# A 3x2x3 block product for q, v and k of a head pair, in place of three two-level 2x2x2 products, from the fourth image on

## The chip, the core and the metric

The kernel runs on one core of a Trainium2 chip. The metric is the device time of one launch in microseconds (us), the median of several runs. The engines of the core work side by side, each through its own queue in order: TensorE (PE) multiplies, VectorE (DVE) and ScalarE (ACT) do elementwise work and empty PSUM, GpSimd (POOL) and SyncE (SP) mostly issue transfers (DMAs). All numbers are fp32.

## The reference

For each of 16 images `x` of 512 channels by 1024 positions:

```python
xn  = group_norm(x, 8 groups) * gamma + beta
qkv = einsum('oc,bchw->bohw', qkv_w, xn) + qkv_b     # 1536 x 512 weights
q, k, v -> 4 heads of 128 channels each
attn = softmax(q . k / sqrt(128))                    # 1024 x 1024 per head
out  = proj_w @ (attn . v) + proj_b                  # 512 x 512 weights
return x + out
```

Per image that is three products of 512 x 512 by 512 x 1024 for q, k and v, four heads of attention, and a fourth such product for the projection.

## The kernel before

**Steps and half steps.** The work is a row of 512 steps: image b, head h, step j of 8 (one block of 128 keys). A step has two halves of 512 queries. In each half PE does one score product (`score`, L1004, 128x512 columns), one weighted sum of the step before (`weighted_sum`, L1101, 128x512), and then the units of a linear product that `plan_head` (L1306) has laid into that half (`halfway`). ACT makes the exponentials (L1010), DVE adds them up for the denominators (`running_sum`, L1023 and L1025). What is made one image ahead: in head 2 of image b the q and k of heads 0 and 1 of image b+1, in head 3 its v, in head 0 of image b+1 the q and k of its heads 2 and 3, in head 1 the projection of image b.

**A linear product before.** `two_levels` (L608) applies a 2x2x2 scheme of 7 products (Winograd's form of Strassen's) twice. The outer level cuts 512 x 512 weights and 512 x 1024 data into 2 x 2 blocks of 256 x 256 and 256 x 512; `OUTER` orders its 7 products into groups of 2, 2, 2 and 1 that share PSUM banks. The inner level (`strassen`, L555) does each outer product as 7 products of 128 x 128 weights by 256 columns (L696, two instructions each, as for every fp32 product here). A unit is one inner product of the whole group; a group has 7 units, in the order p1, p2, p6, p5, p7, p4, p3. The q and k of a head pair are one such product (its weights are the 256 rows of q above the 256 of k), v another, the projection a third.

**Around the units.** Weights of a group come from DRAM by SP (`group_weights`, L429, two buffers of each of two tiles). The inner sums t1 to t4 of the data blocks are made by DVE for the first use (`make_sum`, L661), sent to DRAM by POOL (L667) and loaded again by SP for the two later products (L681, L764). PSUM is emptied by ACT copies (L569 for p1, u2 and u3, L723 for c21) and by DVE additions (L725 for c11, c22, c12). DVE then adds the outer results (L779), writes q and k with their bias (L860), or v with its bias (L918), which it transposes in 32 x 32 blocks (L921); v goes through DRAM by POOL to its last layout (L929, L934). Outer sums of the data are L346, for x and for the projection's input.

**Banks.** PSUM has two banks `x` and two `y` for the linear products, two for scores, two for the weighted sums. In a group p1, p6, p7 and p4 accumulate in one `x` bank, p2 has a `y` bank, p5 and p3 another; so p6 can start when ACT has copied p1, p7 when it has copied u2, p4 when it has copied u3, and p3 when DVE has made c22.

**Order.** The order of each engine's instructions is fixed when the program is built, from the order in which the code emits them and the priorities that it gives (`tc.high_priority`, `tc.issue_after`).

## Time and profile before

| | us |
|---|---|
| median of 3 runs (3135.09 to 3135.28) | 3135.15 |
| span of the profiled execution, first to last instruction | 3133.4 |
| PE busy in it | 3128.2 |
| DVE busy | 2671.6 |
| ACT busy | 1450.0 |
| POOL busy | 513.4 |

The profile page lists one execution. No time outside the first and the last instruction of that execution is given, so its own time is the span; the runs' median is 1.75 us above it. A row of a group has line, engine, operation, output<-input, shape and count, busy time and mean duration of one. A row of a timeline has the start in us, how long the merged instructions took, and their count; consecutive instructions of an engine overlap at their ends, so the distance from start to start is what one of them costs in a full queue. A row of a table by stretches has the busy time of PE, PE's weight loads, DVE, ACT and POOL, the granted clock, the share of the DMA engines and GB/s. One head of a middle image takes 48.6 us, one image 194.5 us.

### The profile page before, as it was taken

How to read it: one execution, taken by the hardware profiler on the slowest of the kernel's cores; microseconds unless marked ns; L12 is line 12 of the kernel's file. 1: busy time of each engine (PE TensorE's matmuls, PEld its weight loads, DVE VectorE, ACT ScalarE, POOL GpSimd, SP SyncE). 2: the span in 40 equal slices, each digit the busy share in tenths (PEclk: the TensorE clock that was granted, in tenths of full speed). 3: DMA queues.
4: the chain of work that ended last, by engine and by line, in shares of the span. 5: the costliest groups of instructions: out<-in, count | busy, mean ns of one | idle time of the engine just before them, and what ended most of it. 6: DMA issues, size and time to landing. Idle time of an engine off the chain costs nothing.

```text
span 3133.4 us, 34161 instructions
## 1 busy us (share of the span) xinstructions
PE 3128.2 (100%) x10418; PEld 2201.9 (70%) x10418; DVE 2671.6 (85%) x4721; ACT 1450.0 (46%) x2663; POOL 513.4 (16%) x923
## 2 busy tenths in 40 slices
PE   9999999999999999999999999999999999999999
PEld 7567777777777777777777777777777777777765
DVE  9988889788897888978799787997879978799787
ACT  3545435354354543545435454453534535345433
POOL 0121121111211112111121101212012120121200
PEclk9999999999999999999999999999999999999999
DMA  5554554545555455454554545555455554555641
GB/s 178 173 188 152 195 175 165 163 152 192 172 169 165 146 197 171 164 169 144 198 170 166 170 143 193 168 176 167 145 187 173 174 173 140 182 171 178 189 133 45
DMA packets 210362, 522.57 MB, mean 167 GB/s; under 512 B 32368, under 2 KB 65776, under 8 KB 210176
## 3 DMA queue, kind: packets, MB, share of 16 engines
q1 hardware_dynamic: 132320, 278.26, 28.7%
q0 software_dynamic: 65184, 207.75, 19.5%
q10 hardware_dynamic: 12672, 34.35, 3.3%
q8 instruction: 85, 1.39, 0.2%
q14 instruction: 101, 0.83, 0.1%
HBM read 387.07 MB, written 133.17 MB: 166 GB/s over the span
## 4 chain that ended last, share of the span: by engine, by line
PE 100%; DVE 0%; issue 0%
PE s L1004 28%; PE po L1101 28%; PE qk_x L696 12%; PE qk_y L696 9%; PE pp_x L696 6%; PE v_x L696 6%; PE pp_y L696 4%; PE v_y L696 4%; PE v_x L878 0%; PE warm L1393 0%; PE v_y L878 0%; PE lx L1208 0%; PE lv L1208 0%; PE v_z L878 0%; PE last_x L696 0%; PE lz L1208 0%
## 5 line engine op out<-in xcount | busy, mean ns | idle before, releaser
L1004 PE MATMUL s<-qk,qk 128*128 128x512 f32 x2048 | 1045.6, 592 | 0.0
L1101 PE MATMUL po<-p,v 128*128 128x512 f32 x2048 | 1045.4, 592 | 0.0
L1010 ACT ACTIVATE p<-s 128x512 f32<-128x512 f32 x1024 | 610.7, 596 | 877.5 <-PE s L1004 857.8
L1101 PEld LDWEIGHTS po<-p,v 128*128 128x128 f32 x2048 | 616.2, 301 | 375.2 <-issue 258.1
L1025 DVE TENSOR_TENSOR tot<-tot,p 128x1024 f32<-128x1024 f32 (+1 forms) x408 | 472.0, 1157 | 136.2 <-ACT p L1010 134.6
L1004 PEld LDWEIGHTS s<-qk,qk 128*128 128x128 f32 x2048 | 389.0, 190 | 68.9 <-issue 13.6
L696 PEld LDWEIGHTS qk_x<-qk_t,w 128*128 128x128 f32 x1344 | 254.9, 190 | 152.2 <-issue 95.2
L696 PE MATMUL qk_x<-qk_t,w 128*128 128x256 f32 x1344 | 352.4, 379 | 0.0
L569 ACT COPY qk_u<-qk_x 128x512 f32<-128x512 f32 (+1 forms) x256 | 136.4, 533 | 233.8 <-PE qk_x L696 232.7
L929 POOL DMA_DIRECT2D vd<-vu x120 | 66.6, 555 | 959.3 <-DVE vu L921 959.1
L725 DVE TENSOR_TENSOR qk_r<-qk_y,qk_u 128x512 f32<-128x512 f32 (+1 forms) x256 | 157.3, 615 | 35.0 <-ACT qk_u L569 21.8
L980 POOL DMA_DIRECT2D out_y<-y x120 | 65.4, 545 | 645.3 <-DVE groups L304 401.3
L725 DVE TENSOR_TENSOR v_r<-v_y,v_u 128x512 f32<-128x512 f32 (+1 forms) x120 | 75.8, 632 | 107.7 <-ACT v_u L569 77.4
L667 POOL DMA_DIRECT2D kept_t<-qk_t x240 | 130.2, 544 | 215.8 <-DVE qk_t L661 190.2
L696 PE MATMUL pp_x<-pp_t,w_proj 128*128 128x256 f32 x630 | 165.3, 379 | 0.0
L696 PE MATMUL v_x<-v_t,w_v 128*128 128x256 f32 x630 | 165.3, 379 | 0.0
L696 PEld LDWEIGHTS pp_x<-pp_t,w_proj 128*128 128x128 f32 x630 | 119.7, 190 | 62.5 <-issue 35.9
L696 PEld LDWEIGHTS v_x<-v_t,w_v 128*128 128x128 f32 x630 | 119.7, 190 | 59.0 <-issue 34.4
L934 POOL DMA_DIRECT2D v<-vd x240 | 140.4, 592 | 68.1 <-issue 37.5
L696 PE MATMUL qk_y<-x,w 128*128 128x256 f32 x512 | 142.1, 379 | 0.0
L860 DVE SCALAR_TENSOR_TENSOR qk<-qk_r,qkb_sb,qk_r 128x512 f32<-128x512 f32 x192 | 137.3, 743 | 1.7
L921 DVE STREAM_TRANSPOSE vu<-vt 128x512 f32<-128x512 f32 x120 | 134.7, 1123 | 0.8 <-DMA vd<-vu 0.8
(259 smaller groups left out, 4413.9 us busy)
## 6 DMA issues: line engine op xcount, KB each, us to landing
w<-kept SPq DMA_DIRECT2D x90, 512.0 KB, 3.9
kept_t<-qk_t POOLq DMA_DIRECT2D x180, 256.0 KB, 2.7
v_t<-kept_t SPq DMA_DIRECT2D x180, 256.0 KB, 2.8
w<-kept SPq DMA_DIRECT2D x90, 384.0 KB, 3.4
rinv<-row ACTq DMA_DIRECT2D x63, 512.0 KB, 4.7
x<-in_x POOLq DMA_DIRECT2D x60, 512.0 KB, 5.0
vd<-vu POOLq DMA_DIRECT2D x120, 256.0 KB, 2.8
v<-vd POOLq DMA_DIRECT2D x240, 128.0 KB, 4.0
```

The costliest lines, as they stand in the source:

```text
L569: nc.scalar.copy(t[n][:, :width], t["x"][:, :width])
L667: nc.gpsimd.dma_start(t, to)
L696: latest["product"] = nc.tensor.matmul(acc[:, ts(i, Q)], have["w"][t][:, i, slot, :], inner(i, bn), start=(first and i == 0), stop=True, s ...
L725: latest["outer"] = nc.vector.tensor_add(dst, view(a), view(c))
L860: return nc.vector.scalar_tensor_tensor(st[b, h][:, ts(half, HALF)], a, qkb_sb[:, i : i + 1], c, ALU.add, ALU.add)
L921: nc.vector.transpose(u.rearrange("p (q i j) -> p j q i", q=n, i=BLK), t.rearrange("p (j q i) -> p j q i", q=n, i=BLK),)
L929: nc.gpsimd.dma_start(rows[which][ts(h, P), :], u)
L934: nc.gpsimd.dma_start(vs[b, pair][ts(q, BLK), half].rearrange("m h (k i) j -> m (h k) (i j)", k=n), rows[which].rearrange("(k m) (q e) -> ...
L1004: latest["score"] = nc.tensor.matmul(sc, ks[b, h][:, ts(j, P)], qs[b, h][:, ts(half, HALF)], start=True, stop=True)
L1010: exps[s] = nc.scalar.activation(ps[s][:, ts(half, HALF)], sc, AF.Exp, scale=SCALE)
L1025: added[b, h, j] = nc.vector.tensor_add(tot[b, h][:, i], tot[b, h][:, i], ps[s][:, i])
L1101: summed = nc.tensor.matmul(po[half], v_block(b, h, j), ps[s][:, i], start=(j == 0), stop=(j == NB - 1),)
```

## The change

For images 3 to 15 (`OLD = 3`) the new function `thirds(b)` takes the place of `qk_groups` and `v_groups`. For each of the two head pairs the 256 rows of q, of v and of k are three blocks of weights over two blocks of inner channels (3 x 2), and the image is two blocks of channels by three pieces of 342 columns that overlap by one column (2 x 3, starts 0, 341 and 682). A scheme of 15 outer products (`FORMS_A`, `FORMS_B`, and the sums in `combine`) stands for the 18 of the plain block product. Each outer product is done by the same inner `strassen` with columns of 171 in place of 256. The 15 are ordered in 8 groups (`THIRDS`: seven of 2, one of 1); two head pairs make 16 groups and 112 units, laid over 48 half steps, 2, 3 and 2 to a half, from head 2 of image b-1 to the end of head 0 of image b, and one unit in its head 1. Before, each of these heads had 28 units for its 16 half steps.

- DVE makes the sums of data blocks (`make_forms`) and the inner sums (`make_sum`) for pair 0, POOL sends both to DRAM, SP loads both for pair 1.
- ACT empties p1, u2, u3 and c21 as before; where a block carries a bias (`BIASED`) the group's copy is split in two instructions of 171.
- Sums of weights for the 15 products are made once (`lay_builder`, `form_steps`, `inner_steps`) during images 0 and 1, and those of pair 1 during image 3 (`sum_weights`).
- x, q and k tiles are joined in pairs, and the SBUF set aside for descriptors of DMAs is 4096 bytes a partition.

Images 0, 1 and 2, the projection and the attention are as before. Counted in the two programs, one middle image has 49 x 3 products of 256 columns for q, k and v before and 210 of 171 columns after. Its other instructions for q, k and v:

| engine, what | before | after |
|---|---|---|
| DVE sums of data blocks | 8 of 512 | 11 of 684 |
| DVE inner sums | 56 of 256 | 20 of 342, 20 of 171 |
| DVE emptying PSUM | 27 of 512, 9 of 256 | 42 of 342, 6 of 171 |
| DVE outer results | 9 of 1024 | 24 of 684 |
| DVE q and k written | 16 of 512 | 8 of 684 |
| DVE v with bias / transposed | 8 of 512 / 8 of 512 | 12 of 342 / 8 of 512 |
| ACT emptying PSUM | 36 of 512, 12 of 256 | 32 of 342, 56 of 171, and 8 of 342 that write q and k |
| sums and forms to DRAM, MB | 3.7 | 9.1 |
| the same loaded again, MB | 7.3 | 9.1 |
| weights loaded, MB | 9.6 | 13.8 |

The core of the diff:

```diff
+THIRDS = ((7, 8), (5, 2), (3, 4), (0, 1), (11, 6), (13, 10), (9,), (14, 12))
+W3 = 342
+S3 = (0, 341, 682)
+H3 = W3 // 2
...
+BIASED = {0: (0, -1), 5: (2, 1), 14: (0, 1), 12: (2, 1)}
+HOMES = "ABABABCABABABACB"
+OLD = 3
...
-    xpool = ctx.enter_context(tc.tile_pool(name="x", bufs=NCC))
+    xpool = ctx.enter_context(tc.tile_pool(name="x", bufs=KC))
-    qkpool = ctx.enter_context(tc.tile_pool(name="qk", bufs=4))
+    qkpool = ctx.enter_context(tc.tile_pool(name="qk", bufs=PAIRS))
-    opool = ctx.enter_context(tc.tile_pool(name="o", bufs=HEADS + 1))
+    opool = ctx.enter_context(tc.tile_pool(name="o", bufs=HEADS + 2))
...
+        def make_forms(G):
+            p, g = parts(G)
+            if p or g not in FORMS_B:
+                return
+            n = size(G)
+            forms[G] = tpool.tile([P, KC, 2, W3], F32, tag="f", bufs=3, name=f"f_{b}_{G}")
...
+            for i, (f, op, a, c) in enumerate(FORMS_B[g]):
+                made[f] = forms[G][:, :, i, :]
+                eng = nc.vector
+                (eng.tensor_add if op == "+" else eng.tensor_sub)(made[f], of(a), of(c))
...
+            nc.gpsimd.dma_start(t, forms[G][:, :, :n, :])
...
+        def load_sum(G, m):
+            g = G % count
+            nc.sync.dma_start(sum_tile(G, m), inner_kept[b, g, m])
...
+        def evict(dst, src, row, G):
...
+            if not any(f in BIASED for f in group):
+                nc.scalar.copy(dst, src)
+                return
+            for i, f in enumerate(group):
+                if f not in BIASED:
+                    nc.scalar.copy(dst[:, i, :], src[:, i, :])
+                    continue
+                m, sign = BIASED[f]
+                nc.scalar.activation(
+                    dst[:, i, :], src[:, i, :], AF.Identity, bias=column(m, p, row, sign)
+                )
...
+            def mm(acc, j, start):
+                an, bn = FACTORS[j]
+                t, slot = SLOTS[an]
+                for i in range(n):
+                    moving = sums[G, bn][:, i, :] if bn[0] == "t" else block(
+                        G, i, int(bn[1]) - 1, int(bn[2]) - 1
+                    )
+                    latest["product"] = nc.tensor.matmul(
+                        acc[:, ts(i, H3)], wts[G, t][:, i, slot, :], moving,
+                        start=(start and i == 0), stop=True, skip_group_check=True,
+                    )
...
+                after_(G + 1, 0, load_weights, 0)
+                after_(G + 1, 3, load_weights, 1)
+                after_(G, 0, sum_weights)
+                after_(G + 1, 1, make_forms)
+                after_(G + 1, 2, make_sum, "t1")
+                after_(G + 1, 3, make_sum, "t2")
+                after_(G + 1, 4, make_sum, "t3")
+                after_(G + 1, 5, make_sum, "t4")
+                after_(G + 2, 3, load_forms)
...
+        units = staggered(
+            [group_units(G) for G in range(2 * count)], [4 * G for G in range(2 * count)]
+        )
+        sizes = (2, 2) + (2, 3, 2) * 15 + (1, 2)
...
+        if flow and h != 1:
+            if h == 0:
+                late["heads"] = True
+            spread(plan, [None] * 37, 0, NB)
+            halfway.extend(flow[:16])
+            del flow[:16]
...
+        elif b + 1 >= old:
+            if h == 2:
+                flow.extend(thirds(b + 1))
+                spread(plan, [None] * 37, 0, NB)
+                halfway.extend(flow[:16])
+                del flow[:16]
...
-    nc = bacc.Bacc("TRN2", target_bir_lowering=False, num_devices=1)
+    nc = bacc.Bacc(
+        "TRN2", target_bir_lowering=False, num_devices=1, dynamic_dma_scratch_size=4096
+    )
```

## The prediction, as it was put on record

> **What bounds the kernel now.** I read the page first (busy times, slices, chain), then the table of waits of PE, then stretches of one head, then timelines for what one instruction costs.

> ```profile
> span 3133.4 us, 34161 instructions
> PE 3128.2 (100%) x10418; PEld 2201.9 (70%) x10418; DVE 2671.6 (85%) x4721; ACT 1450.0 (46%) x2663; POOL 513.4 (16%) x923
> PEclk9999999999999999999999999999999999999999
> PE 100%; DVE 0%; issue 0%
> PE s L1004 28%; PE po L1101 28%; PE qk_x L696 12%; PE qk_y L696 9%; PE pp_x L696 6%; PE v_x L696 6%; PE pp_y L696 4%; PE v_y L696 4%; PE v_x L878 0%; PE warm L1393 0%; PE v_y L878 0%; PE lx L1208 0%; PE lv L1208 0%; PE v_z L878 0%; PE last_x L696 0%; PE lz L1208 0%
> PE warm L1393 <- DVE avg L251: 1.6, 1, 1.6
> ```

> The chain is PE from end to end at full clock, and the last row is PE's whole table of waits: 1.6 us, at the start. So PE's own stream is the time, and whatever it loses or gains counts in full. But DVE is at 85%, so there is little room before it takes over. By head of one image (head 1, 2, 3 and the next image's 0), then the whole image, with columns PE, PE's loads, DVE, ACT, POOL, clock, DMA share, GB/s:

> ```profile
> 1055.90:1104.50 48.60, 48.60 (x164) 34.40 (x163) 43.18 (x87) 33.49 (x67) 4.41 (x8) 1.00 0.40 128
> 1104.50:1153.10 48.60, 48.60 (x163) 34.54 (x162) 44.92 (x80) 19.11 (x34) 10.76 (x20) 1.00 0.64 213
> 1153.10:1201.70 48.60, 48.60 (x163) 34.55 (x162) 33.94 (x53) 19.31 (x35) 4.41 (x8) 1.00 0.46 145
> 1201.70:1250.40 48.70, 48.70 (x164) 34.62 (x164) 43.65 (x73) 19.17 (x34) 13.17 (x24) 1.00 0.62 191
> 1104.50:1299.00 194.50, 194.50 (x649) 138.15 (x648) 165.67 (x290) 91.11 (x168) 32.73 (x59) 1.00 0.53 169
> ```

> DVE works 44.9 of 48.6 us in head 2 and PE still does not wait. That a queue at 92% holds nobody up is the best evidence for the order of this kernel.

> **PE's stream.** What one pass costs (an fp32 product is two passes), from start to start. First loads of weights and products in the opening, then a half step of image 5:

> ```profile
> 8.46 2.09 PEld L1393 LDWEIGHTS warm<-avg 128*128 128x128 f32 x18
> 10.47 0.30 PEld L1423 LDWEIGHTS pm<-mv,avg 128*128 128x128 f32 x2
> ...
> 25.37 7.07 PE L878 MATMUL v_x<-wv_a,xt 128*128 128x256 f32 x32
> 32.28 1.89 PE L878 MATMUL v_y<-wv_s,x 128*128 128x256 f32 x8
> ...
> 1163.44 1.02 PE L1004 MATMUL s<-qk,qk 128*128 128x512 f32 x2
> 1164.30 1.02 PE L1101 MATMUL po<-p,v 128*128 128x512 f32 x2
> ```

> 256 columns: (32.28 - 25.37) / 32 = 0.2159 us. 512 columns: 0.86 / 2 = 0.430. 128 columns: (10.47 - 8.46) / 18 = 0.1117, each with a load of its own. No row has 171 columns. From 256 and 512 a column costs (0.430 - 0.2159) / 256 = 0.00084, so 171 columns come to 0.2159 - 85 x 0.00084 = 0.145. The line between 128 and 256 gives 0.147, pure proportion 0.144. I take 0.145, because 128 columns may already be limited by the load. One image then has 210 x 2 x 0.145 = 60.9 us where it had 147 x 2 x 0.2159 = 63.5: 2.6 less, and 13 images (3 to 15) give **-33.5 us** (-22 by 0.147, -39 by 0.144). The saving is 4.6% of columns (35910 for 37632), and a fixed cost of 6 ns a pass would be enough to eat it.

> [...]

> **VectorE.** What its operations cost in a full queue:

> ```profile
> 1108.30 0.75 DVE L661 TENSOR_TENSOR qk_t<-x 128x256 f32<-128x256 f32 x2
> 1108.97 0.75 DVE L661 TENSOR_TENSOR qk_t<-x,qk_t 128x256 f32<-128x256 f32 x2
> ...
> 1137.15 1.22 DVE L1114 TENSOR_TENSOR o<-o,rinv 128x1024 f32<-128x1024 f32 x1
> 1138.29 1.22 DVE L779 TENSOR_TENSOR qk_r<-qk_r,qk_r 128x1024 f32<-128x1024 f32 x1
> 1139.42 0.68 DVE L346 TENSOR_TENSOR o<-o 128x512 f32<-128x512 f32 x1
> 1140.03 1.22 DVE L779 TENSOR_TENSOR qk_r<-qk_r,qk_r 128x1024 f32<-128x1024 f32 x1
> ...
> 1146.82 0.75 DVE L860 SCALAR_TENSOR_TENSOR qk<-qk_r,qkb_sb 128x512 f32<-128x512 f32 x1
> 1147.48 0.42 DVE L725 TENSOR_TENSOR qk_r<-qk_y,qk_p 128x256 f32<-128x256 f32 x1
> ```

> 256 elements 0.335, 512 0.60, 1024 1.135, and 512 with a bias 0.66. By lines between them 684 is 0.78, 342 is 0.424 (0.484 with bias) and 171 is 0.247. With the counts of the two programs, before: 8 x 0.60 + 56 x 0.335 + (27 x 0.60 + 9 x 0.335) + 9 x 1.135 + 24 x 0.66 = 68.8 us an image. After: 11 x 0.78 + 20 x 0.424 + 20 x 0.247 + (42 x 0.424 + 6 x 0.247) + 24 x 0.78 + 8 x 0.78 + 12 x 0.484 = 72.0. So +3.2, 168.9 us of an image of 191.9. That does not bound the image, but its spread changes: bias and copies of q and k move from the ends of products into the flow, and sums of blocks pile up in head 2, where the pair 0 forms are made. Adding these costs along the changed program's DVE queue gives for heads 0 to 3 41.4, 44.8, 46.5 and 32.5 us, beside PE's 46.3, 49.8, 48.9 and 46.9. The same sum for the old program is 161.9 an image where the row has 165.7, so I raise it by 1.023: **47.6 of 48.9 us in head 2**.

> I followed the two queues by hand through that head. A half step with two units takes 2 x 0.86 + 2 x 0.58 = 2.88 us, with three 3.46. The first product of the third group stands 17.3 us after the head's start. It needs both sums of `f_2`, and DVE, held by c12 of the first group until 12.8, has 4.7 us of work up to the second of them: done at 17.5. With a semaphore that is 0.4 us of wait, once an image, or **+5** for 13. Everywhere else in the head the sums come 0.4 to 6 us ahead. At the start of head 3 the c12 of the fifth group comes between 0.7 us early and 1.2 late; I take nothing. Bounds of the waits: 0 to 1.2 us an image.

> **ScalarE.** Its rows for copies:

> ```profile
> L569 ACT COPY qk_u<-qk_x 128x512 f32<-128x512 f32 x192 | 112.6, 587 | 190.8 <-PE qk_x L696 190.8
> L569 ACT COPY qk_u<-qk_x 128x256 f32<-128x256 f32 x64 | 23.8, 372 | 43.0 <-PE qk_x L696 41.8 <-DVE qk_r L725 1.1
> ```

> From these 342 is 0.44 and 171 is 0.30: 40 x 0.44 + 56 x 0.30 = 34.4 us for 36 x 0.587 + 12 x 0.372 = 25.6, +9 in 91 of 192. It hides behind PE. The nearest deadline is copy u3: p7 ends 2.3 us ahead of p4, and an exponential (0.60) and a split copy (0.60) fit in it. If the cover went, each of 16 groups would pay up to 0.3.

> **Transfers.** Rows for what SP loads, and what it waits for:

> ```profile
> w<-kept SPq DMA_DIRECT2D x90, 512.0 KB, 3.9
> ...
> SPq L429 <- PE qk_y L696: 1110.9, 198, 10.8
> ```

> SP already waits for buffers and not the reverse. Now a weight buffer comes free at the end of p5 and its next content is due one group and one half step later, 11.5 us, for 3.9. In head 2 there are 3.8 MB more of sums and forms and 1.8 MB more of weights: (213 x 48.6 + 5600) / 48.9 = 326 GB/s, and at 0.64 for 213 a share of 0.98. That is at the edge, but what is late there is wanted a head later, and the weights could take double. I count nothing; a stall is in the rival below. [...]

> **Once.** The sums of weights fall into images 0, 1 and 3. Image 3 makes those of pair 1 in head 0: 32 operations of at most 0.335, 3.4 us above a middle image by the same sum, (41.4 + 3.4) x 1.023 = 45.8 of 46.3 us. Between 0 and 10 us for all of it; I take **+3**, near the empty end, since no engine is over its head's time.

> **Sum.** -33.5 + 5 + 3 = -25.5 us: span 3133.4 to 3107.9, and the median, 1.75 above it, 3135.15 to 3109.7, say **3110**.

> **Rivals.**
> - *The waits eat the gain.* Each image loses 1.2 to 3 us at several of the tight places (c12 before p5, forms before p1, c22 before p3, ACT held by a DVE result that it must write out). For: before, DVE waits for PE and PE never for DVE, while here sums and copies of one group are wanted within 3 half steps. Against: the walk found one such place. 13 x 1.2 to 3 gives 3120 to 3141.
> - *VectorE becomes the bound of head 2, and it is slower.* An operation that uses the result of the one ahead of it cannot overlap it:

> ```profile
> L661 DVE TENSOR_TENSOR qk_t<-x,qk_t 128x256 f32<-128x256 f32 x256 | 105.3, 429 | 2.2 <-PE qk_x L696 0.7
> ```

>   That is 0.43 in place of 0.335. If some 55 of head 2's short operations paid 0.09 more, it would need 46.5 + 5 = 51.5 us and more where PE has 48.9; late transfers would act alike. The point from which it decides is 2.6 us an image. At 3.6 us: 13 x 3.6 = 47, so 3135 - 33.5 + 47 + 3 = 3151. Against: the 92% of the row above.
> - *The shorter pass is not shorter*, because of odd starts of rows or loads that show. At the floor of today's pass, 420 x 0.2159 - 63.5 = +27 us an image, 3490; with loads in the open, 420 x (0.112 + 0.145) - 63.5 = +44 an image, about 3710. Against: 128 columns at 0.1117.

> **Chances.** The forecast with waits of 0 to 1.2 us an image, 3101 to 3120: 0.50. Waits eat the gain: 0.13 below 3129 and 0.10 within 0.2% of 3135 (6.3 us, about what a measurement can tell from no change). VectorE bounds head 2: 0.21. Passes not shorter: 0.06. So faster 0.63, same 0.10, slower 0.27. The range goes from 3100, no wait at all, to 3150, the upper rival's middle; some 0.18 lie outside, nearly all above.

> **What would show it.** Right: the 171-column passes (L1168) 0.145 apart, a middle image of about 192.3 us, PE's waits a few tenths an image, at the first product of a group that uses `f`. Wrong: passes at 0.147 or more; in head 2 DVE without idle time and PE waiting on L1043, L1089 or L1192; landings of weights (L1108) above 9 us, with PE waiting on DMAs; or ACT idle for DVE ahead of exponentials.

## The result and the profile after

The changed kernel takes 3231.7 us (median; 3214.12 to 3236.49) where the kernel before took 3135.14 in the same runs: 1.0298 times as long (95% interval 1.0272 to 1.0323). It is slower by 97 us, and the prediction had 25 us less. The page of the changed kernel, with the rows that answer to those of before:

```profile
span 3234.8 us, 40108 instructions
...
PE 3143.8 (97%) x12056; PEld 2271.2 (70%) x12056; DVE 2758.0 (85%) x4959; ACT 1565.7 (48%) x3288; POOL 676.6 (21%) x1225
...
PE 53%; DVE 18%; DMA 12%; issue 4%; ACT 1%; POOL 1%; SPq 0%; ACTq 0%; DVEq 0%; POOLq 0%
```

The chain was 100% PE and is now half of it. The table of PE's waits had one row of 1.6 us. Now (total, times, longest):

```profile
PE t_x L1168 <- DMA w<-kept: 37.0, 20, 4.9
PE t_y L1168 <- DVE r L1192: 23.3, 24, 4.1
PE pp_x L742 <- ACT pp_u L613: 8.2, 15, 0.6
PE qk_y L742 <- DVE qk_r L771: 5.8, 4, 2.1
```

The first row is the weights of the block product that SP loads, the second DVE's emptying of PSUM. Heads 0 to 3 of image 5, then their sum (columns as in the prediction: PE, loads, DVE, ACT, POOL, clock, DMA share, GB/s):

```profile
1053.40:1099.80 46.40, 46.40 (x197) 34.88 (x196) 37.30 (x58) 21.84 (x49) 0.79 (x2) 1.00 0.57 186
1099.80:1151.80 52.00, 50.57 (x171) 35.42 (x171) 46.26 (x91) 35.06 (x70) 14.26 (x26) 1.00 0.67 217
1151.80:1201.40 49.60, 49.49 (x213) 37.33 (x212) 49.53 (x94) 21.79 (x49) 18.99 (x35) 1.00 0.94 273
1201.40:1252.20 50.80, 47.77 (x201) 35.39 (x200) 36.83 (x60) 21.48 (x49) 10.54 (x19) 1.00 0.97 285
sum 198.80, PE 194.23 PEld 143.02 DVE 169.92 ACT 100.18 POOL 44.59; mean PE 48.56 PEld 35.76 DVE 42.48 ACT 25.04 POOL 11.15
```

Read against PE's work by the prediction (46.3, 49.8, 48.9, 46.9), head 0 is right to 0.1, and the three others are long by 2.2, 0.7 and 3.9. In the same way for the whole run: cut at the first score product of each head, the excess over PE's work is 74 us in the 13 heads 3 (14 of them in image 2), 28.5 in the heads 1, 11 in the heads 2, 0.7 in the heads 0. Images 0 and 1 and the first half of image 2, which have no block product, are 18.4 longer than before, start and end 2.6. Together 135.5; less the 33.5 that PE's passes save, that is 102, and the two spans differ by 101.4.

A head 3 that is worse, in image 8, and what its transfers took from issue to landing:

```profile
1803.00:1858.50 55.50, 50.51 (x200) 36.92 (x199) 37.35 (x61) 21.65 (x49) 10.57 (x19) 0.94 0.90 263
```
```profile
w<-kept SPq DMA_DIRECT2D x5, 512.0 KB, 8.9
w<-kept SPq DMA_DIRECT2D x5, 384.0 KB, 7.2
...
row<-r ACTq DMA_DIRECT2D x1, 4.0 KB, 7.5
```

The prediction shows 3.9 for the larger of these loads of weights before the change. PE's own rows there, with a wait for weights:

```profile
1843.07 0.74 PE L1168 MATMUL t_x<-s_t,w 128*128 128x171 f32 x4
1848.68 1.48 PE L1168 MATMUL t_x<-f,w 128*128 128x171 f32 x4 [4.87 <-DMA w<-kept]
1849.96 1.91 PE L1580 MATMUL s<-qk,qk 128*128 128x512 f32 x2
1851.66 1.92 PE L1677 MATMUL po<-p,v 128*128 128x512 f32 x2
```

Two passes of 512 cost 1851.66 - 1849.96 = 1.70 here and 0.86 elsewhere: after the wait PE runs at half clock, by its rows until 1854.49, 5.8 us from the wait's end. The granted clock is 0.94 in the row of the head and 0.995 over the run, so an estimate for all such stretches is 0.005 x 3235 = 16 us.

### The profile page after: what moved, and what is told of

The parts are those of the page before. It is cut to its first block, busy times and chain, and to the rows that moved or that the text cites. A ratio compares the mean times of both kernels' runs of the same rounds, so it can differ in the third digit from the quotient of the medians.

```text
span 3234.8 us, 40108 instructions
## 1 busy us (share of the span) xinstructions
PE 3143.8 (97%) x12056; PEld 2271.2 (70%) x12056; DVE 2758.0 (85%) x4959; ACT 1565.7 (48%) x3288; POOL 676.6 (21%) x1225
## 3 DMA queue, kind: packets, MB, share of 16 engines
q1 hardware_dynamic: 200512, 410.48, 41.8%
## 4 chain that ended last, share of the span: by engine, by line
PE 53%; DVE 18%; DMA 12%; issue 4%; ACT 1%; POOL 1%; SPq 0%; ACTq 0%; DVEq 0%; POOLq 0%
PE s L1580 15%; PE po L1677 15%; PE t_x L1168 9%; PE t_y L1168 7%; DMA w<-kept 6%; PE pp_x L742 4%; PE pp_y L742 3%; DVE tot L1601 3%; DMA s_t<-kept_t 3%; DVE vu L982 2%; DVE r L1192 2%; DMA row<-r 1%; DVE r L1256 1%; DVE s_t L1089 1%; DVE y L1552 1%
## 5 line engine op out<-in xcount | busy, mean ns | idle before, releaser
L1168 PEld LDWEIGHTS t_x<-s_t,w 128*128 128x128 f32 x2340 | 397.0, 191 | 227.9 <-issue 150.0
L1168 PE MATMUL t_x<-s_t,w 128*128 128x171 f32 x2340 | 444.8, 309 | 0.8 <-DMA w<-kept 0.8
L1095 POOL DMA_DIRECT2D kept_t<-s_t x416 | 224.1, 541 | 341.8 <-DVE s_t L1089 222.7
L1256 DVE TENSOR_TENSOR r<-r,r 128x684 f32<-128x684 f32 x286 | 243.1, 865 | 6.4 <-issue 0.2
L1192 DVE TENSOR_TENSOR r<-t_y,t_u 128x342 f32<-128x342 f32 (+1 forms) x416 | 201.3, 484 | 41.3 <-ACT t_u L1127 31.5
L1168 PE MATMUL t_y<-f,w 128*128 128x171 f32 x1144 | 203.3, 310 | 21.7 <-DVE r L1192 21.6
L1168 PEld LDWEIGHTS t_y<-f,w 128*128 128x128 f32 x1144 | 175.3, 190 | 27.7 <-DVE r L1192 27.7
L1192 DVE TENSOR_TENSOR r<-t_y,t_p 128x342 f32<-128x342 f32 x208 | 101.1, 486 | 108.1 <-ACT r L1131 94.2
L1127 ACT COPY t_u<-t_x 128x342 f32<-128x342 f32 x260 | 108.4, 417 | 167.6 <-PE t_x L1168 150.4
L742 PEld LDWEIGHTS pp_x<-pp_t,w_proj 128*128 128x128 f32 x630 | 117.5, 190 | 77.2 <-issue 32.5
L1168 PE MATMUL t_y<-s_t,w 128*128 128x171 f32 x780 | 150.2, 309 | 2.9 <-DVE r L1192 1.5
L1168 PE MATMUL t_x<-f,w 128*128 128x171 f32 x572 | 114.5, 316 | 32.9 <-DMA w<-kept 32.9
## 6 DMA issues: line engine op xcount, KB each, us to landing
w<-kept SPq DMA_DIRECT2D x187, 512.0 KB, 5.4
rinv<-row ACTq DMA_DIRECT2D x63, 512.0 KB, 5.8
x<-in_x POOLq DMA_DIRECT2D x60, 512.0 KB, 7.9
```

The costliest lines, as they stand in the source:

```text
L742: latest["product"] = nc.tensor.matmul(acc[:, ts(i, Q)], have["w"][t][:, i, slot, :], inner(i, bn), start=(first and i == 0), stop=True, s ...
L1095: nc.gpsimd.dma_start(t, to)
L1127: nc.scalar.copy(dst, src)
L1168: latest["product"] = nc.tensor.matmul(acc[:, ts(i, H3)], wts[G, t][:, i, slot, :], moving, start=(start and i == 0), stop=True, skip_grou ...
L1192: nc.vector.tensor_add(dst, view(a), view(c))
L1256: (nc.vector.tensor_add if add else nc.vector.tensor_sub)(at(o), a, c)
```

## The experiments

Every run is the changed kernel but for its edit. Runs that leave out loads, sums, transposes or the normalisation compute another result and serve only to find causes. The theory to start with: **transfers** make head 3 late. The rival: **VectorE**, which has 49.53 of 49.60 us in head 2, is behind, and all that follows is late with it. Mean heads of images 4 to 14, and medians, in us:

| | head 0 | 1 | 2 | 3 | image | median |
|---|---|---|---|---|---|---|
| before | 48.6 | 48.7 | 48.6 | 48.6 | 194.5 | 3135.1 |
| PE's work, by the prediction | 46.3 | 49.8 | 48.9 | 46.9 | 191.9 | |
| the change | 46.4 | 52.0 | 49.8 | 51.8 | 200.0 | 3231.7 |
| half of the weights | 46.4 | 52.1 | 49.6 | 48.0 | 196.1 | 3178.1 |
| half of the transfers | 46.3 | 52.1 | 49.6 | 47.2 | 195.2 | 3162.0 |
| the same, half of the sums | 46.3 | 52.1 | 49.6 | 46.9 | 194.9 | 3156.0 |
| half of the sums, stored twice | 46.4 | 52.0 | 57.4 | 55.1 | 210.9 | 3369.6 |
| sums and forms by POOL | 46.4 | 52.1 | 49.8 | 48.5 | 196.8 | 3186.3 |
| x by SP | 46.4 | 51.8 | 49.7 | 48.1 | 196.0 | 3179.3 |
| x by SP, forms late | 46.4 | 51.8 | 49.4 | 48.5 | 196.1 | 3175.0 |
| forms ahead of sums | 46.4 | 52.0 | 49.7 | 54.1 | 202.2 | 3251.0 |
| both queues, o earlier | 46.4 | 51.8 | 49.7 | 47.3 | 195.1 | 3165.2 |
| no transposes | 46.4 | 50.9 | 50.2 | 52.2 | 199.7 | 3218.4 |
| no normalisation | 46.4 | 51.7 | 55.5 | 48.2 | 201.8 | 3249.7 |
| neither of the two | 46.4 | 50.2 | 54.6 | 48.8 | 200.0 | 3225.5 |

### The parts that are not the block product

```diff
-OLD = 3
+OLD = 16
```

> OLD = 16: no image uses the block product and nothing of its weights is made; what stays of the change are the joined tiles for x, q and k, one more tile of o and the smaller descriptor ring. Transfer theory (the loss is made where heads 2 and 3 move 270 to 290 GB/s) and VectorE theory (the loss is made where head 2 has 49.5 of 49.6 us of DVE) both expect 3135, within 6 us, since neither load is there. The rival, that the ring or the joined tiles cost something by themselves, expects some part of the 97 us here: 3150 or more.

3136.61 us, 1.0005 times before (0.9996 to 1.0015), every middle image 194.5. The joined tiles and the smaller ring cost nothing that can be measured.

### Fewer bytes

```diff
-                nc.sync.dma_start(wts[G, t][:, :n], store3[p, g, t])
+                nc.sync.dma_start(wts[G, t][:, :1], store3[p, g, t][:, :1])
...
-                        acc[:, ts(i, H3)], wts[G, t][:, i, slot, :], moving,
+                        acc[:, ts(i, H3)], wts[G, t][:, 0, slot, :], moving,
```

> Of each group's weights in the block product only the first half is loaded and used for both of its products, from image 4 on; instructions of all engines are the same (the exponential of those images is scaled down). 6.4 MB less an image. Transfer theory: the waits of PE on w<-kept (37.0 us, longest 4.9) go, head 3 comes from 48.5 to 55.5 us close to its 46.9 of PE work, and 12 images win some 4 to 5 us each with the half clock behind the waits: about 3231 - 55 = 3175 (3160 to 3195). VectorE theory: head 3 is late because VectorE is, and the time stays within 10 us of 3231. Both expect head 1 to keep its 52.0.

3178.06 us (1.0133, 1.0116 to 1.0150): 54 less, as the transfer theory had it to 3 us, and head 3 from 51.8 to 48.0. Next, the sums and forms of pair 1 as well:

```diff
-            nc.sync.dma_start(sum_tile(G, m), inner_kept[b, g, m])
+            nc.sync.dma_start(sum_tile(G, m)[:, :1], inner_kept[b, g, m][:, :1])
...
-            nc.sync.dma_start(forms[G][:, :, :n, :], inner_kept[b, g, "f"])
+            nc.sync.dma_start(forms[G][:, :, :1, :], inner_kept[b, g, "f"][:, :, :1, :])
```

> As the run with half the weights, and pair 1 also loads only the first of the two blocks of each sum and form (and uses it for both products); some 4 MB less an image on top. Transfer theory: the same as with half the weights or up to 15 us less, 3150 to 3180, and SP's waits at L1099 on its own loads go. VectorE theory: within 10 us of 3231. Head 1 keeps 52.0 by both; if it falls, the theory that head 1's excess of 2.2 us is VectorE's fails.

3161.96 us (1.0086, 1.0069 to 1.0103). Of PE's waits in this run the row for the weights is gone, the two of DVE and ACT are left:

```profile
PE t_y L1168 <- DVE r L1192: 13.1, 18, 1.6
PE pp_x L742 <- ACT pp_u L613: 8.3, 15, 0.6
```

So head 3 was the transfers', with VectorE's queue untouched. One sign of the expectation failed: SP still stands at L1099, for 432 us in all, but its longest wait there is 2.5 us where the change has 6.1. What stays is head 1, head 2, and what is paid once: even with no wait of PE for weights the kernel is 27 us slower than before.

### Fewer sums for VectorE

```diff
-                    nc.vector.tensor_sub(to, of(a), of(c))
+                    nc.vector.tensor_sub(to[:, :1], of(a)[:, :1], of(c)[:, :1])
...
-                    for i in range(n):
+                    for i in range(1):
...
-            nc.gpsimd.dma_start(t, to)
+            nc.gpsimd.dma_start(t, to[:, :1].to_broadcast((P, n, H3)))
```

> VectorE makes only the first of the two blocks of each sum t1 to t4 for pair 0; the store writes it twice, so all transfers keep their size. 16 of some 45 operations on the way go from 342 to 171 columns (0.424 to 0.247 us by the prediction's prices) or from two to one, 5.5 us an image less, about 4 of them in head 2 and 1.5 in head 3. VectorE theory: head 2's queue comes from 49.5 to 46 of 49 us, heads 1 to 3 lose 3 to 5 us in all, 13 times: 3231 - 40 to 65 = 3165 to 3190. Transfer theory: only head 2 gains 0.7 us, 3220 to 3231, and head 3 still has its waits on w<-kept.

3369.55 us (1.0747): both theories missed it, since the edit was not the clean one that it was meant to be. Its waits, of PE and of ACT, and landings in image 5:

```profile
PE t_x L1168 <- DMA w<-kept: 74.6, 35, 6.5
PE t_x L1168 <- ACT t_u L1131: 56.8, 13, 5.4
...
ACT t_u L1134 <- DMA row<-r: 88.7, 13, 7.9
```
```profile
kept_t<-s_t POOLq DMA_DIRECT2D x28, 171.0 KB, 13.2
...
kept_t<-s_t POOLq DMA_DIRECT2D x4, 85.5 KB, 11.7
```

The stores that read one block twice move as many bytes but land after 13.2 us in image 5, where the plain ones of the change took 7.3 in the same image (11.5 and 7.4 over the two runs). Not all of that is the store's own: the 85.5 KB stores of the group of one have the same form in both runs, stand in the same queue, and went from 5.4 to 11.7. In this image the packets of GpSimd's queue were as many as in the change (5920, 19.07 MB), but took 33.2% of the 16 engines' 217 us for 30.4% of 199. Why is not shown. With that, transfers got worse and not better. The ACT row shows a second way in which they are felt: `spread_inverse` sends 4 KB of reciprocals to DRAM and reads them back spread out, both from ACT's queue, and ACT stands until the 4 KB have landed: 13 times, 7 us each, with PE's copies behind it. So this run fits the transfer theory, but it changed two things at once and decides nothing by itself. The clean form, with only the first block stored, on top of half the transfers:

> As the run with half the transfers (3162), and VectorE makes only the first block of each sum for pair 0, and only that is stored: 5.5 us less of VectorE an image in heads 2 and 3, no transfer grows. If what is left of head 2 (49.6 for 48.9 of PE work) is VectorE's, head 2 comes to 48.9 and head 3 stays 46.9 to 47.3: 12 or 13 x 0.7 to 1.0 = 8 to 13 us less, 3149 to 3154. If head 2's 0.7 comes from ScalarE or elsewhere, 3160. Head 1 keeps 52.0 by both.

3156.03 us (1.0067, 1.0050 to 1.0084), 6 less, which is neither of the expected times. Head 2 stayed at 49.6: its 0.7 is not the amount of VectorE's sums. The gain is mostly the last 0.3 of head 3. Where the 0.7 arises can be read from the change, 4 us into head 2 of image 5 (it begins at 1151.80), DVE and then PE:

```profile
1155.06 1.22 DVE L1601 TENSOR_TENSOR tot<-tot,p 128x1024 f32<-128x1024 f32 x1
1156.19 0.58 DVE L1092 TENSOR_TENSOR s_t<-x 128x171 f32<-128x171 f32 x2
```
```profile
1155.54 1.02 PE L1677 MATMUL po<-p,v 128*128 128x512 f32 x2
1156.67 0.53 PE L1168 MATMUL t_y<-s_t,w 128*128 128x171 f32 x2
```

PE is free at 1155.54 + 0.86 = 1156.40 and starts at 1156.67, since the first inner sums stand in DVE's queue behind what head 1 left there: the projection's output and the sums for the denominators. In the eleven middle heads 2 of the change some 0.55 us are lost 5 to 6 us into the head, and 0.68 with half of the sums. So it is VectorE after all, by the place of the first sums in its queue and not by how many there are. This is read from the rows; no run moved them.

### Which queue

```diff
-            nc.sync.dma_start(sum_tile(G, m), inner_kept[b, g, m])
+            nc.gpsimd.dma_start(sum_tile(G, m), inner_kept[b, g, m])
...
-            nc.sync.dma_start(forms[G][:, :, :n, :], inner_kept[b, g, "f"])
+            nc.gpsimd.dma_start(forms[G][:, :, :n, :], inner_kept[b, g, "f"])
```

> The loads of sums and forms of pair 1 go out from POOL's queue and not from SP's, ahead of which the weights stand in line; bytes and sizes stay. If the weights are late because they stand behind those loads in SP's queue, PE's waits on w<-kept (37 us) fall below 10 and the time to 3180 to 3195, as with half the weights. If the 16 engines themselves are full in heads 2 and 3 (share 0.94 to 0.97), nothing is won: 3220 to 3245, and waits on s_t<-kept_t or on v's way take the place.

3186.26 us (1.0167, 1.0150 to 1.0184) with all bytes moved: 45 less. SP's waits in the change, then SP's and PE's in this run:

```profile
SPq L1108 <- PE t_y L1168: 754.4, 238, 6.4
SPq L1099 <- PE t_x L1168: 404.9, 244, 6.1
```
```profile
SPq L1108 <- PE t_y L1168: 1492.8, 347, 8.9
...
PE t_x L1168 <- DMA w<-kept: 5.3, 6, 1.5
```

In the change SP stands 405 us in front of the tiles of sums (L1099), with the weights (L1108) behind it in line. Without that it stands at the weights' own buffer and asks the moment it is free. The same bytes, asked for from another queue, are less late: PE's waits for weights fall from 37.0 to 5.3 us, so the bytes alone do not decide. The total of SP's waits is no measure of it, as the run with half of the transfers shows. No run here tells apart what asking earlier and what a further queue gained.

Then the load of x, which in the change stands in POOL's queue behind the loads of v (issued 9.9 us into head 1):

```diff
-                eng = nc.gpsimd if b > 0 else nc.scalar if half == 1 else nc.sync
+                eng = nc.sync if b > old else nc.gpsimd if b > 0 else (
+                    nc.scalar if half == 1 else nc.sync)
```

> From image 4 on the next image's x is loaded through SP's queue and not POOL's, where it stood behind the eight loads of v (image 5: issued 9.9 us into head 1, normalisation 7 us later than before the change). Theory that the end of head 1 is late through x: the copies pp_u come on time, PE's waits on L613 (8.2 us, 15 times) go, head 1 comes from 52.0 to 50.8 to 51.0; 11 x 1.1 = 12 us less, 3219, unless head 3's waits on transfers take it. Rival: the end of head 1 is late because VectorE is late since the four transposes; head 1 stays at 52.0 and the time within 6 us of 3231.

3179.28 us (1.0149, 1.0132 to 1.0166). The expectation was wrong both ways: head 1 gained 0.2, and head 3 gained 3.7, which nobody expected. In this kernel the first forms of pair 1 had also moved four places ahead in SP's order, so two runs took these apart:

```diff
+            with tc.issue_after(late["sum", "t3"].ins) if G == 9 else nullcontext():
                 nc.sync.dma_start(forms[G][:, :, :n, :], inner_kept[b, g, "f"])
```

> As the run with x on SP's queue (3179), but the load of the first form pair that pair 1 needs is issued behind the third of the four sums of the group before, the place that it has in the change (one place in SP's order differs, all other queues are the same as with x on SP). If the place of that load in SP's line is what made head 3 late, head 3 goes back to 50 to 55 us and the time to 3220 to 3235. If it was x (earlier statistics, VectorE less behind in head 2), 3175 to 3185.

3175.03 us (1.0124): it is x, not the place of the forms. The reverse, x where the change has it and SP's order alone altered:

```diff
-    5: (8,), 7: (9,), 8: (10,), 9: (11,), 10: (12,), 11: (13,), 12: (14, 15),
+    7: (9,), 8: (10,), 9: (11,), 10: (12,), 11: (13,), 12: (14, 15),
...
+                after_(G + 2, 0 if G == 7 else 3, load_forms)
+                if G == 7 and k == 0:
+                    for m in ("t2", "t1", "t3", "t4"):
+                        load_sum(8, m)
```

> The change with x on POOL as it was; only SP's order is different: the first weights of the last group of pair 0 and the first forms of pair 1 go ahead of the four sums of the group before. If SP's line is the cause, 3175 to 3200 with PE's waits on w<-kept under 15 us, and head 1 still at 52.0. If x is the cause, 3220 to 3235.

3250.95 us (1.0364): 19 worse, outside both expected ranges. So SP's order alone brings nothing, and why an early x helps head 3 is not settled. A row that goes with it: the last big store of forms, issued in the first 10 us of head 3 of image 5 in the change, and in the last 10 us of head 2 with x early:

```profile
keptf<-f POOLq DMA_DIRECT2D x1, 684.0 KB, 10.6
```
```profile
keptf<-f POOLq DMA_DIRECT2D x1, 684.0 KB, 4.5
```

This holds in all eleven middle images: that store is issued 6.8 to 7.9 us into head 3 in the change and in the run with SP's order alone altered, and 0.4 to 2.1 us before head 3 in both runs with x early. That the time is won because the stores of pair 0 then no longer meet the first loads of pair 1 is argued from these, not shown. All three at once, with the differences of the projection's input asked for one step earlier:

```diff
-                plan[6].append(lambda: o_blocks(b - 1))
-                plan[6].append(lambda: sums_of_b(ob[b - 1]))
+                at_ = 5 if b >= old else 6
+                plan[at_].append(lambda: o_blocks(b - 1))
+                plan[at_].append(lambda: sums_of_b(ob[b - 1]))
```

> Loads of sums and forms on POOL's queue, x on SP's, and from image 3 on the differences of o for the projection are made one step earlier in head 0 (step 5 for 6), so that VectorE's queue at the end of head 0 is shorter when the four transposes come. If these are three separate causes they add up: 3186 - 12 - 11 x 1 = 3160 to 3170, head 1 at 49.8 to 50.2, head 3 at 47 to 49 as with the loads on POOL alone. Faster than before the change it would only be with head 3 at 46.9 as well and the 27 us paid once gone. Rival: POOL's and SP's queues hold each other up (v behind sums, w_proj behind x), 3186 or more.

3165.15 us (1.0102, 1.0085 to 1.0118). That the time lies in the expected range is luck: head 1 stayed at 51.8 where 49.8 to 50.2 was expected, so the earlier differences gained nothing, and what made up for it is head 3, at 47.3 for 48.5 with the loads on POOL alone. Head 3 of image 10 in this run:

```profile
2154.70:2201.60 46.90, 46.90 (x200) 35.37 (x199) 36.14 (x59) 21.64 (x49) 23.13 (x43) 1.00 1.01 307
```

The DMA engines are full for the whole head (share 1.01, 307 GB/s) and PE does not wait once. So a full share alone is no loss; head 3 of image 5 in the change, at 0.97, was 3.9 us over PE's work.

### Head 1

Where head 1 of image 5 begins (1099.80) in the change, DVE and PE:

```profile
1097.22 3.93 DVE L982 STREAM_TRANSPOSE vu<-vt 128x512 f32<-128x512 f32 x4
1100.98 1.23 DVE L1601 TENSOR_TENSOR tot<-tot,p 128x1024 f32<-128x1024 f32 x1
...
1102.44 0.51 DVE L1192 TENSOR_TENSOR r<-t_y,t_u 128x342 f32<-128x342 f32 x1
```
```profile
1103.01 0.85 PE L1168 MATMUL t_y<-f,w 128*128 128x171 f32 x4 [0.77 <-DVE r L1192]
```

Four transposes of v stand ahead of the addition that frees PE's bank for its last unit. Left out for pair 1:

```diff
-        nc.vector.transpose(
+        if b >= old and pair:
+            u = t
+        else:
+            nc.vector.transpose(
```

> The four transposes of v for pair 1 are left out from image 3 on (v is stored as it is); they end head 0 and begin head 1. VectorE theory for head 1: PE's wait of 1.2 us at its start goes, VectorE is 4 us earlier in the whole head and the waits at its end go too, so head 1 comes from 52.0 to 49.8 to 50.3: 13 x 2 = 26 us less, 3205. Rival: only the wait at the start goes and ScalarE's normalisation makes the end late by itself, 51.0, 3218. Second rival: head 3 takes back what head 1 gains, since transfers bind over the whole image; then within 8 us of 3231 with head 3 longer by 2.

3218.40 us (1.0259), head 1 at 50.9: the first rival's number. For the rest, the normalisation of the next image, which stands among ACT's copies at the end of head 1:

```diff
                         for c in range(KC * r, KC * r + KC) for half in range(NH2)
+                        if not (b + 1 > old and True)
```

> The change, but from image 4 on the eight normalising operations of ScalarE (0.73 us each, in head 1 of the image before) are left out; the raw x goes into the products. If ScalarE's block is what makes the end of head 1 late, PE's waits on L613 (8.2 us, 15 times) go and head 1 comes from 52.0 to 50.8 to 51.0; if not, 52.0. What head 3 does with it is not foreseen: 3205 to 3235.

> As the run without the normalisation, and without the four transposes of v of pair 1 (as in the run that left out these alone, head 1 50.9). If the two are all that head 1's 2.2 us consist of, head 1 comes to PE's work, 49.8 to 50.0; if a third cause is left (VectorE's own backlog of sums for the projection and the forms of the first group), 50.4 or more.

Without the normalisation alone head 1 is 51.7 and the time 3249.7, above the expected range: PE waits for DVE at the same place instead of for ACT. Without both head 1 is 50.2, between the two numbers expected, and the time 3225.5; PE's work is 49.8. So, taken out in this order, VectorE's backlog from the transposes is 1.1 of the 2.2, ACT's block behind it 0.7 more, and 0.4 stays open. Both runs lose some 5 us in head 2, by the same row of ACT as above (here without the normalisation alone); why it comes up in these two runs is not shown:

```profile
ACT t_u L1134 <- DMA row<-r: 74.5, 12, 7.5
```

### What is paid once

```diff
-OLD = 3
+OLD = 15
```

> OLD = 15: the weights of the block product are made in images 0 to 2 as before, but only the last image uses them. It shows what is paid once. By the changed kernel's heads: +4.5 us in image 0, +10.2 in image 1, +3.8 in head 0 of image 2, and some 10 to 15 in the heads in which the one image runs by thirds and sums its pair 1 weights: 3160 to 3175. The prediction's own term for it was +3 once, so 3136. Transfer theory in addition: the head after the one that makes the forms is the late one, with PE waiting on weights that come in pieces.

3163.57 us (1.0092, 1.0076 to 1.0109). Images 0 to 2 pay 19.5 us while they make the weights, and head 3 of image 14, where the first pair 1 sums its weights, takes 56.5. In the last head of image 0, ACT and DVE wait:

```profile
ACT p L1586 <- DVE a_o L1413: 9.9, 2, 6.9
...
DVE a_o L1413 <- DMA a_o<-in_qkv_wT: 5.8, 1, 5.8
```

Two causes were tried: the builder's sums on GpSimd, and its transfers from SP with the sums further behind their loads.

```diff
-                eng = nc.vector
+                eng = nc.gpsimd
                 made[f] = slot(f)
...
-            inner_weights(w, n)
+            inner_weights(w, n, nc.gpsimd)
```

> OLD = 15 as in the run that uses the weights in the last image alone (3163.6), with the builder's 76 sums of weights (25 us by the prediction's price of 0.335) on GpSimd in place of VectorE. If the 19 us that images 0 to 2 pay are VectorE's, they nearly go: 3145 to 3150, image 1 at 195 to 198 for 205.6. If they are paid for buffers or transfers of the builder, 3160 to 3165. If GpSimd and VectorE hold each other up or POOL's stores of y and v come late behind it, more than 3170.

3171.16 us (1.0115), with the row of the sums:

```profile
L1413 POOL TENSOR_TENSOR a_o<-a_o 128x256 f32<-128x256 f32 x28 | 22.6, 823 | 45.5 <-DMA a_o<-in_qkv_wT 38.1 <-DMA kepta<-a_o 7.2
```

The heads 0 of images 1 and 2 came from 55.1 to 50.1 and from 51.8 to 48.6, so there the loss is VectorE's work; the heads 3 of images 0 and 1 got worse by 4 each and head 2 of image 1 by 6, behind slower sums (0.82 us mean duration, where the same line on VectorE had 0.42), for which exponentials on ACT waited 16.4 us.

```diff
-        for i, step in zip((0, 2, 3, 5, 6), form_steps(*chunks.pop(0))):
+        for i, step in zip((0, 4, 5, 6, 7), form_steps(*chunks.pop(0))):
...
-                nc.scalar.dma_start(forms_kept[p, c][:, i:e], t)
+                nc.sync.dma_start(forms_kept[p, c][:, i:e], t)
```

> OLD = 15 as in the run that uses the new weights in the last image alone (3163.6). The builder's loads and stores go out from SP and not from ScalarE's queue, and its sums stand four half steps behind their load (two before) or six (five before). The work is the same. If images 0 to 2 pay 19 us because ScalarE stands waiting for VectorE's sums ahead of exponentials (9.9 us in head 3 of image 0) and VectorE for the builder's loads (5.8 and 4.5 us), they pay 5 to 10: 3150 to 3156, head 3 of image 0 at 49 to 51 for 53.9. If they pay for VectorE's 25 us of work, 3160 to 3166.

3159.36 us (1.0090): images 0 to 2 pay 16.2 for 19.5, in one profile each of kernels whose runs spread over 7 and 13 us. So the waits for transfers are at most the smaller part. What makes the heads 3 of images 0 and 1 late stays open. In head 3 of image 2 of the change, the longest of its heads (61.0 for 46.9), the rows do show it. DVE, then PE:

```profile
640.90 0.42 DVE L1449 TENSOR_TENSOR w<-w 128x256 f32<-128x256 f32 x1 [7.69 <-DMA w<-in_qkv_wT]
...
643.51 0.51 DVE L1192 TENSOR_TENSOR r<-t_y,t_u 128x342 f32<-128x342 f32 x1
```
```profile
644.07 1.51 PE L1168 MATMUL t_y<-f,w 128*128 128x171 f32 x4 [4.09 <-DVE r L1192]
```

DVE stands 7.69 us for a load that a sum of weights of pair 1 needs, and the emptying of PSUM behind that sum in its queue is late by it. PE waits 4.09 us and then runs at half clock (0.85 us for a pass of 512); earlier in the same head it waits 3.8 us for weights, with half clock again (0.85). Together that is some 13 of the 14 us. With the queues of the runs above as well:

> Thirds from image 3 on, with all at once: sums and forms loaded by POOL, x by SP, the builder's transfers on SP and its sums further behind their loads. If the causes add up: 3165 less 8 to 15 us of the builder, 3150 to 3157. It would still be above 3135, since a middle image is at 194.5 (head 1 at 51.8 for 49.8 of PE's work), the same as before the change. If SP's line gets too long with the builder in it, 3165 or more.

3166.27 us (1.0107): no better than without the builder's edit, and above the expected 3150 to 3157. No version that uses the block product from image 3 on beat the kernel before. The best that keeps the whole computation (3165.15) has middle images of 195.1 on average, five of the eleven at 194.5 or 194.6, which is what the kernel before takes, and pays 22 us in images 0 to 2.

## Why the prediction was wrong

- **PE's stream (-33.5): right.** From the timeline of the change, ahead of head 1:

```profile
1096.32 0.74 PE L1168 MATMUL t_x<-s_t,w 128*128 128x171 f32 x4
1096.90 0.74 PE L1168 MATMUL t_y<-s_t,w 128*128 128x171 f32 x4
1097.48 1.02 PE L1580 MATMUL s<-qk,qk 128*128 128x512 f32 x2
```

  Eight passes in 1.16 us are 0.145 each, and heads 0 and undisturbed heads 3 take 46.4 and 46.9. The rival of passes that are not shorter is out, with loads in the open too: 171 columns at the 0.00084 us of the prediction's rows are an estimated 0.144, which leaves no room in 0.145 us for a weight load of 0.11. In head 0 of image 5 PE is busy for all of the 46.40 us and its loads for 34.88 of them, so they run beside the passes; what lets them do so is not shown.
- **Transfers ("I count nothing"): the step that failed first.** The share in head 2 was forecast at 0.98 and came to 0.94, but by luck: 326 GB/s were forecast and 273 moved, and each byte took more of the engines' time than the prediction had it (0.94 for 273, where it used 0.64 for 213). What failed is the sentence behind the share, that what is late there is wanted a head later and the weights could take double, so that head 3 was priced at PE's work alone. Head 3 had a share of 0.97 itself. Its weights did take double (8.9 in image 8, 5.4 over the run), but they were also asked for late, since SP stands in line for tiles of sums, and their slack was used twice. The prediction's own sign for this, landings of weights near 9 us with PE waiting on DMAs, is what came. This is some 60 of the 74 us in the heads 3, half clock included; 14 are in image 2, with what is paid once. A queue of loads was treated as a bandwidth, and not as a line with a head.
- **Waits (+5): wrong in place and size.** The walk went through head 2 and the start of head 3, and found 0.4 us at 17.3 us into head 2, half of it for a semaphore, a price for which it shows no row. In the rows above where PE did wait for VectorE, it started 0.05 and 0.06 us after the operation's end (644.07 for 643.51 + 0.51, 1103.01 for 1102.44 + 0.51). No such wait as the forecast one shows at its place in the middle images. Head 2 lost 0.7 to 0.9, most of it 5 to 6 us after its start, behind what head 1 had left in VectorE's queue. The larger part, 2.2 us in each head 1 (28.5 in all), came where pair 1 ends and the projection begins, which the walk left out: the prediction's costs per head had VectorE at 44.8 of 49.8 there, and the mean hid four transposes in a row.
- **VectorE's load: nearly right for the image, low for head 2.** 47.6 of 48.9 in head 2 was forecast, 49.53 of 49.60 measured; 169.9 us an image for 165.7, so +4.2 and not +3.2. Head 2 lost under 1 us all the same, and 0.7 also with 1.8 us less work for VectorE there, so its load is not what bounds the head. The 0.43 that the rival sets against 0.335 is a mean duration, and rows of that line that use no earlier sum have 0.41 to 0.42 as well; 0.335 is a distance from start to start. The price is about right even so: where a sum uses the one directly ahead of it, at 1129.77 us in the kernel before, that distance is 0.44.
- **ScalarE: hidden in heads 0, 2 and 3, as far as its work goes.** In head 1 its block of normalisation is part of the 2.2 us. Not considered was that it stands still for a 4 KB transfer in its own queue: 19.5 us in 6 waits in the change.
- **Once (+3): wrong.** Some 18 us in images 0 and 1 and the first half of image 2, and 14 in head 3 of image 2. The prediction and the section on the change put pair 1's 32 sums of weights into image 3; 12 of them stand in head 3 of image 2, and one waits there 7.69 us for its load. The 20 in head 0 of image 3 cost nothing (46.4), as its sum had it. It went by totals again, where single operations were in the way.
- **The rivals.** The one that ended slower priced 3.6 us an image and said that late transfers would act alike. They did, at 8 us an image over PE's work; its own cause, VectorE as the bound of head 2, did not. Its chance of 0.21 was too small, and no rival reached the time that came: the slowest but for the longer passes stood at 3151. By its own terms the upper end of the waits rival is 3135 - 33.5 + 39 + 3 = 3144, not 3141.

## What to carry to other kernels

When a change adds loads to a queue, walk that queue entry by entry, with what each waits for and what stands behind it: the same bytes cost 45 us less from another queue. One head at a DMA share of 1.01 was free of waits, and one at 0.97 was 3.9 us over PE's work: the share by itself did not tell. And where the gain is 1% of an image, walk every seam between stages once, and price what is made once by where it stands, not by its sum.
